# A two-layer MetaFormer with a selective scan: last states enter by a ScalarE product, GpSimd makes one C product more, deeper row buffers, later gates

## The chip, the cores and the metric

The kernel runs on one core of a Trainium2 chip. The metric is the device time of one launch in microseconds (us), the median of several runs. The engines are TensorE (PE in the profile, PEld for its weight loads), VectorE (DVE), ScalarE (ACT), GpSimd (POOL) and SyncE (SP), which issues nearly all transfers here. Each engine works through its own queue in order; between engines, semaphores tell when data is ready or a buffer is free.

## The reference, cut to what matters

The input is two images of 96 channels, 128 x 128 pixels. Layer 0 normalizes each pixel over the channels, runs four Mamba blocks (over rows, rows backwards, columns, columns backwards), joins their outputs and adds them; layer 1 has a 3 x 3 convolution instead. After each comes a small quantized feed-forward part. Nearly all of the time is spent in the Mamba blocks, of which this is the core:

```python
dt = jax.nn.softplus(dt_raw @ dt_w.T + dt_b)
A = -jnp.exp(A_log)
def step(h, t):
    dt_t, u_t, B_t, C_t = t
    dA = jnp.exp(dt_t[:, :, None] * A)
    h = dA * h + dt_t[:, :, None] * B_t[:, None, :] * u_t[:, :, None]
    y = jnp.einsum('bds,bs->bd', h, C_t)
    return (h, y)
_, ys = jax.lax.scan(step, h0, xs)
y = ys.transpose(1, 0, 2) + Dp * xc
y = y * jax.nn.silu(z)
return y @ outp_w.T
```

There are 16384 tokens per sequence, 192 inner channels and 16 states per channel.

## The kernel before, in words

For each of the two images: `normalize` (layer norm, and a copy of the image in row order and in column order to DRAM), `mamba`, then `ffn_and_conv`. The change touches `mamba` alone, and one argument where the program is made.

`mamba` treats the four directions as two pairs (one row and one column direction each, both forwards or both backwards). A pair has 2 x 192 = 384 channels, which fill three groups `g` of 128 partitions. Tokens are cut into 32 tiles of 512; one tile of one pair is a *step*, so there are 64 steps per image and 128 in the run. Within a step, a *unit* is one group and two states: `units` has 3 x 8 = 24 of them, numbered here 0 to 23; units 0, 8 and 16 start a group. Two units share a *quad* of four states.

For one unit the engines do this:
- SP loads the rows of B and of C for a quad from a DRAM scratch (`bcd`), broadcast to 128 partitions: 1 MB each (`row_tile`, L331 to L338). B rows are fetched 3 quads ahead (`B_AHEAD`), C rows 2 (`C_AHEAD`), in buffers of one more than that: 4 and 3.
- GpSimd multiplies the B rows by dt·u for a whole quad, in place (`b_part`, L339). Where the step is not the first of a sequence (i > 0), it also adds to the first token's column what the last step's states leave: `entry` (L303) makes exp(dt·A) of the first token on ScalarE, L342 multiplies it by the last states `hst`, L343 adds it into the row.
- ScalarE makes dA, two exponentials of 512 tokens into PSUM (`decay`, L349). The pool `ps_w` has three such buffers of two banks each; y and a tile for everything else take the two banks left.
- DVE runs two scans, one per state (`scan`, L353), then multiplies the states by the C rows (L441). In the units of `BY_POOL`, 0, 4, 8, 12, 16 and 20, the scan writes its states into the row tile instead of dA, and GpSimd makes the C product (`by_pool`, L360).
- ScalarE saves the last token's states (L442), and TensorE sums the products over states by multiplying with an identity into y (`sums`, L357). At the end of a group DVE multiplies y by the gate `sz` (`gated`, L364).

What a step needs beforehand (convolution, gates, dt, the scratch rows) is the `prologue` of the step before: a list `at` of small parts, each with a unit number counted from 24 units before the step, and a place: 0 is before scan 0 of the unit, 1 is after scan 1. On ScalarE these are copies out of PSUM, and three activations that need other tables and so have two table loads each: silu of the gates behind unit 7 (L259), silu of the convolution before unit 11, softplus of dt behind unit 17 (L293).

The order on every engine is the order in which the program is written (`in_order`). The loop over k, one pass per unit, sets it: transfers and GpSimd's B product for later units, parts with place 0, scan 0 of unit k, `behind(k - 1)` (C product, state copy, sums, and in a group's first unit the gate of the group before, L446, and the first matmul into a new y, L448), dA of unit k + 2, scan 1 of unit k, the C rows' transfer, parts with place 1. GpSimd's C product of unit k is registered for the pass k + 1, its sums for the pass k + 3. With three dA buffers, dA of unit k + 2 goes where that of unit k - 1 was.

## Time and profile before

| | |
|---|---|
| median of 3 runs | 11548.93 us (11548.27 to 11549.71) |
| the profiled execution | 11556.77 us, its span 11555.0 us |
| granted TensorE clock, mean | 0.989 |
| step | about 79.1 us, 128 of them |
| DVE scans (L353) | 6144 of about 1.21 us |
| DVE C products (L441) | 2304 of 1.21 us |
| GpSimd B products (L339) | 1536 of 4.52 us |
| GpSimd C products (L360) | 768 of 2.35 us |
| ScalarE exponentials (L349) | 6144 of 0.69 us |
| ScalarE entry (L303), GpSimd L342 and L343 | 372 of 0.29, 372 of 0.22, 1488 of 0.20 us |
| row transfers | 3072 of 1 MB, 7.4 us from issue to landing (median) |

Times in the profile are counted from the start of the span. A group line gives the line of the kernel, the engine, the operation, output and inputs, how many there are, busy time and the mean of one, then the idle time of the engine just before them and what ended it. In a timeline, "x2" merges two instructions that follow each other; the bracket is the idle time before and what ended it. In a table of stretches each row gives the busy time of each engine in it, then the granted clock, the share of the DMA engines' time, and GB/s.

### The profile page before, as it was taken

Reading aid. Unit: us, or ns where it says so; the run is one execution under the profiler, and the core shown is the slowest. Engines: PE = TensorE matmul, PEld = TensorE weight load, DVE = VectorE, ACT = ScalarE, POOL = GpSimd, SP = SyncE. Lnnn points to the kernel's source line nnn. Section 1 sums busy time; section 2 is a strip of 40 time slices with the busy share of each in tenths; the row PEclk is TensorE's granted clock in tenths of the full one; section 3 lists DMA queues with packets and bytes.
Section 4 is the critical chain, followed back from the end, with each engine's and each line's share of the span. In section 5 each row is a group of like instructions: output and inputs, shape, how many; then the busy total and the mean of one; then the engine's idle time right before and its main releaser. Section 6 shows DMA issues by size and latency. Waiting matters only on the chain. (4 is left out here: it accounts for less than half of the span.)

```text
span 11555.0 us, 94102 instructions
## 1 busy us (share of the span) xinstructions
PE 10435.0 (90%) x24208; PEld 3971.4 (34%) x24208; DVE 10421.6 (90%) x10127; ACT 7901.7 (68%) x13564; POOL 9672.3 (84%) x4700
## 2 busy tenths in 40 slices
PE   7999999999999999989989999999999999999899
PEld 2333333333333333333323333333333333333333
DVE  6999999999999999994469999999999999999944
ACT  6767767677677677665567677677676776776655
POOL 5999999999999999991159999999999999999911
PEclk8999999999999999999989999999999999999999
DMA  7888888888888888880068888888888888888800
GB/s 263 335 329 333 333 332 332 330 331 333 329 332 333 330 331 333 329 322 19 26 243 334 328 331 334 330 333 333 333 331 329 332 332 329 331 333 329 319 13 13
DMA packets 540755, 3416.96 MB, mean 296 GB/s; under 512 B 67532, under 2 KB 68652, under 8 KB 143832
## 3 DMA queue, kind: packets, MB, share of 16 engines
q1 hardware_dynamic: 539960, 3410.16, 76.8%
q8 instruction: 196, 3.21, 0.1%
q14 instruction: 343, 2.81, 0.1%
q0 software_dynamic: 256, 0.79, 0.0%
HBM read 3289.04 MB, written 54.53 MB: 289 GB/s over the span
## 5 line engine op out<-in xcount | busy, mean ns | idle before, releaser
L339 POOL TENSOR_TENSOR row<-dtu,row 128x2048 f32<-128x2048 f32 x1536 | 6948.9, 4524 | 283.3 <-DMA row<-bcd 281.6
L357 PE MATMUL y<-row,ident 128*128 128x512 f32 x12288 | 5690.6, 603 | 700.0 <-DVE row L441 699.9
L353 DVE TENSOR_TENSOR_SCAN da<-da,row 128x512 f32<-128x512 f32 x4608 | 5456.9, 1214 | 38.9 <-ACT da L349 5.2
L349 ACT ACTIVATE da<-dt,amat 128x512 f32<-128x512 f32 x6144 | 4246.9, 691 | 170.2
L357 PEld LDWEIGHTS y<-row,ident 128*128 128x128 f32 x12288 | 2256.8, 190 | 4008.4 <-issue 2243.5
L441 DVE TENSOR_TENSOR row<-da,row 128x1024 f32<-128x1024 f32 x2304 | 2776.7, 1205 | 70.2 <-DMA row<-bcd 70.0
L442 ACT COPY hst<-da 128x2 f32<-128x2 f32 x2304 | 368.9, 160 | 2652.2 <-DVE row L441 2649.3
L360 POOL TENSOR_TENSOR row<-row,row 128x1024 f32<-128x1024 f32 x768 | 1807.4, 2353 | 223.0 <-DVE row L353 147.5
L353 DVE TENSOR_TENSOR_SCAN row<-da,row 128x512 f32<-128x512 f32 x1536 | 1852.4, 1206 | 91.9 <-POOL row L339 84.1
L211 PE MATMUL misc<-xa,inx 96*64 96x512 f32 (+1 forms) x2048 | 946.1, 605 | 50.0 <-ACT mix L239 26.8
L211 PE MATMUL misc<-xb,inx 96*64 96x512 f32 (+1 forms) x2048 | 952.3, 608 | 33.6 <-ACT hst L442 24.2
L564 POOL TENSOR_TENSOR acc<-acc,y 96x512 f32<-96x512 f32 x128 | 147.4, 1151 | 991.5 <-DVE y L563 991.5
L298 POOL TENSOR_TENSOR dtu<-dt,xc 128x512 f32<-128x512 f32 x384 | 487.4, 1269 | 106.0 <-DMA xb<-xnc 99.8
L576 PE MATMUL pc<-pad,kw 96*96 96x512 f32 x1152 | 566.4, 593 | 0.0
L211 PEld LDWEIGHTS misc<-xa,inx 96*64 96x64 f32 (+1 forms) x2048 | 327.3, 165 | 581.2 <-issue 438.0
L448 PE MATMUL y<-xc,dmat 128*128 128x512 f32 x768 | 419.5, 628 | 103.6 <-DVE sz L364 103.6
L374 PE MATMUL misc<-sz,gmat 128*96 128x512 f32 x1024 | 484.1, 595 | 0.0
L284 PE MATMUL misc<-rows,dtw 12*128 12x512 f32 x768 | 434.3, 645 | 50.6 <-ACT dt L289 37.9
L364 DVE TENSOR_TENSOR sz<-y,sz 128x512 f32<-128x512 f32 x384 | 264.6, 689 | 229.5 <-PE y L357 198.0
L136 DVE TENSOR_TENSOR xq<-xm,rs 96x512 fp8e5<-96x512 f32 x128 | 87.9, 687 | 392.2 <-ACT rs L132 392.2
L211 PEld LDWEIGHTS misc<-xb,inx 96*64 96x64 f32 (+1 forms) x2048 | 316.5, 164 | 361.9 <-issue 214.1
L372 PE MATMUL misc<-acc,ident 96*96 96x512 f32 x512 | 387.6, 842 | 57.3 <-ACT sz L247 53.8
(76 smaller groups left out, 7449.9 us busy)
## 6 DMA issues: line engine op xcount, KB each, us to landing
row<-bcd SPq DMA_DIRECT2D x3072, 1024.0 KB, 7.4
xc<-mix SPq DMA_DIRECT2D x256, 128.0 KB, 5.4
sz<-mix SPq DMA_DIRECT2D x256, 128.0 KB, 8.9
xa<-xnr SPq DMA_DIRECT2D x124, 193.1 KB, 8.6
xb<-xnc SPq DMA_DIRECT2D x124, 193.1 KB, 8.7
bcd<-rows SPq DMA_DIRECT2D x128, 128.0 KB, 9.5
acc<-in_x_dram SPq DMA_DIRECT2D x16, 768.0 KB, 5.7
xnr<-xn SPq DMA_DIRECT2D x16, 768.0 KB, 4.3
```

Of the source, the lines that this page charges most:

```text
L211: nc.tensor.matmul(ps[rows, :], w(PAIRS[pi][d], k, lo, hi), src[d][:, k : k + T], **se)
L284: nc.tensor.matmul(d["ps"], w, d["rows"][0 : 2 * RK, :], start=True, stop=True)
L298: nc.gpsimd.tensor_tensor(dtu, d["dt"][:, g, :], d["xc"][:, g, :], ALU.mult)
L339: nc.gpsimd.tensor_tensor(b, d["dtu"][g][:, None, :].broadcast_to((128, 4, T)), b, ALU.mult)
L349: nc.scalar.activation(da[:, j, :], d["dt"][:, g, :], AF.Exp, scale=amat[:, pi, g, s + j : s + j + 1])
L353: nc.vector.tensor_tensor_scan(h[:, j, :], da[:, j, :], b[:, j, :], 0.0, ALU.mult, ALU.add)
L357: nc.tensor.matmul(y, ident, c[:, j, :], start=False, stop=s + j == S - 1)
L360: nc.gpsimd.tensor_tensor(c, h, c, ALU.mult)
L374: nc.tensor.matmul(d["po"], gmat[:, pi, 2 * g - 2 + k, :], d["yg"][g - 1 + k], start=False, stop=k == 1)
L441: nc.vector.tensor_tensor(c, h, c, ALU.mult)
L448: nc.tensor.matmul(y, dmat[:, pi, g, :], d["xc"][:, g, :], start=True, stop=False)
L576: nc.tensor.matmul(pc, kw[:, t, :], rows, start=t == 0, stop=t == 8)
```

## The change

Four things change in `mamba`.

The last states enter elsewhere. `entry`, the tile `enter` and the three lines L341 to L343 are gone. In `decay`, where i > 0, two further ScalarE instructions multiply the first token's dA, in PSUM, by the saved state of that unit; the scan then starts from 1.0 instead of 0.0, so its first product is that value.

`BY_POOL` also holds (1, 4), which is unit 10: seven C products of 24 are GpSimd's.

The row buffers no longer follow from the read-ahead: `ROW_BUFS` gives 5 for B and 4 for C, at read-aheads of 3 and 2 as before. The space that is set aside for the descriptors of GpSimd's transfers goes down to 2048 bytes.

`behind(k - 1)` moves behind scan 1 of unit k where unit k - 1 is the first of a group and in `BY_POOL` (units 0, 8, 16), so the gate and the first matmul into the next y come one scan later, and the state copy behind dA of unit k + 2.

```diff
+ROW_BUFS = (5, 4)
-BY_POOL = tuple((g, s) for g in range(3) for s in (0, 8))
+BY_POOL = tuple((g, s) for g in range(3) for s in (0, 8)) + ((1, 4),)
...
-                    if i > 0:
-                        at += [((20, 24, 29)[g], 1, partial(entry, g))]
...
-                t = gen.tile([128, 4, T], F32, name=f"row{k}", bufs=ahead + 1)
+                t = gen.tile([128, 4, T], F32, name=f"row{k}", bufs=ROW_BUFS[k])
...
-                if i > 0:
-                    if s == 0:
-                        nc.gpsimd.tensor_tensor(enter[:, g, :], enter[:, g, :], hst[:, g, :], ALU.mult)
-                    nc.gpsimd.tensor_tensor(b[:, :, 0], b[:, :, 0], enter[:, g, s : s + 4], ALU.add)
...
-            def decay(pi, d, g, s):
+            def decay(pi, i, d, g, s):
...
+                if i > 0:
+                    for j in range(2):
+                        nc.scalar.activation(da[:, j, 0:1], da[:, j, 0:1], AF.Copy, scale=hst[:, g, s + j : s + j + 1])
                 return da
...
-                nc.vector.tensor_tensor_scan(h[:, j, :], da[:, j, :], b[:, j, :], 0.0, ALU.mult, ALU.add)
+                nc.vector.tensor_tensor_scan(h[:, j, :], da[:, j, :], b[:, j, :], float(i > 0), ALU.mult, ALU.add)
...
+            def begins(k):
+                return 0 <= k < total and units[k % nu][1] == 0 and units[k % nu] in BY_POOL
...
-                if 0 < k <= total:
+                if 0 < k <= total and not begins(k - 1):
                     behind(k - 1)
                 feed_decay(k + AHEAD)
                 if k < total:
-                    scan(1, da, b, hs[k])
+                    scan(steps[n][1], 1, da, b, hs[k])
+                if begins(k - 1):
+                    behind(k - 1)
...
-    nc = bacc.Bacc("TRN2", target_bir_lowering=False, num_devices=1)
+    nc = bacc.Bacc("TRN2", target_bir_lowering=False, num_devices=1, dynamic_dma_scratch_size=2048)
```

More of the change, by code (lines that the diff above doesn't have):

```diff
@@ L194, in mamba @@
             hst = one.tile([128, NG, S], F32, name="hst")
-            enter = one.tile([128, NG, S], F32, name="enter")
             acc_w = acc.rearrange("c (h w) -> c w h", w=W)
@@ L299, in dt_u @@
                     d["dtu"].append(dtu)
-                def entry(g):
-                    nc.scalar.activation(enter[:, g, :], amat[:, pi, g, :], AF.Exp, scale=d["dt"][:, g, 0:1])
                 first = pi == 0 and i == 0
@@ L327, in prologue, with row_tile @@
                 return sorted(at, key=lambda p: p[:3])
-            def row_tile(d, g, s, k, ahead):
-                t = gen.tile([128, 4, T], F32, name=f"row{k}", bufs=ahead + 1)
+            def row_tile(d, g, s, k):
+                t = gen.tile([128, 4, T], F32, name=f"row{k}", bufs=ROW_BUFS[k])
                 src = d["bcd"][k, s // 4] if g == 1 else d["bcd"][k, s // 4, g // 2 : g // 2 + 1]
@@ L336, in row_tile, with b_part @@
                 return t
-            def b_part(i, d, g, s, b):
+            def b_part(d, g, b):
                 nc.gpsimd.tensor_tensor(b, d["dtu"][g][:, None, :].broadcast_to((128, 4, T)), b, ALU.mult)
-                if i > 0:
-                    if s == 0:
-                        nc.gpsimd.tensor_tensor(enter[:, g, :], enter[:, g, :], hst[:, g, :], ALU.mult)
-                    nc.gpsimd.tensor_tensor(b[:, :, 0], b[:, :, 0], enter[:, g, s : s + 4], ALU.add)
-            def decay(pi, d, g, s):
+            def decay(pi, i, d, g, s):
                 da = ps_w.tile([128, 2, T], F32, name="da")
@@ L349, in decay, with scan @@
                     nc.scalar.activation(da[:, j, :], d["dt"][:, g, :], AF.Exp, scale=amat[:, pi, g, s + j : s + j + 1])
-                return da
-            def scan(j, da, b, h):
-                nc.vector.tensor_tensor_scan(h[:, j, :], da[:, j, :], b[:, j, :], 0.0, ALU.mult, ALU.add)
+                if i > 0:
+                    for j in range(2):
+                        nc.scalar.activation(da[:, j, 0:1], da[:, j, 0:1], AF.Copy, scale=hst[:, g, s + j : s + j + 1])
+                return da
+            def scan(i, j, da, b, h):
+                nc.vector.tensor_tensor_scan(h[:, j, :], da[:, j, :], b[:, j, :], float(i > 0), ALU.mult, ALU.add)
             def sums(s, y, c):
@@ L413, in mamba, with fetch @@
             bs, cs, das, hs, quads = {}, {}, {}, {}, {}
-            def fetch(k, n, ahead, m):
+            def fetch(k, n, m):
                 if k < total:
-                    t = row_tile(state[k // nu], *units[k % nu], n, ahead)
+                    t = row_tile(state[k // nu], *units[k % nu], n)
                     m[k], m[k + 1] = t[:, 0:2, :], t[:, 2:4, :]
@@ L425, in feed @@
                     n = k // nu
-                    b_part(steps[n][1], state[n], *units[k % nu], quads.pop(k))
+                    b_part(state[n], units[k % nu][0], quads.pop(k))
             def feed_decay(k):
@@ L430, in feed_decay, with gate_before @@
                     n = k // nu
-                    das[k] = decay(steps[n][0], state[n], *units[k % nu])
+                    das[k] = decay(*steps[n], state[n], *units[k % nu])
             ys = {}
+            def gate_before(k):
+                pn, pu = divmod(k - 1, nu)
+                gated(steps[pn][0], state[pn], units[pu][0], ys.pop(k - 1))
+            def begins(k):
+                return 0 <= k < total and units[k % nu][1] == 0 and units[k % nu] in BY_POOL
             def behind(k):
@@ L444, in behind @@
                     if k > 0:
-                        pn, pu = divmod(k - 1, nu)
-                        gated(steps[pn][0], state[pn], units[pu][0], ys.pop(k - 1))
+                        gate_before(k)
                     y = ps_y.tile([128, T], F32, name="y")
@@ L464, in mamba @@
                 for k in range(ahead):
-                    fetch(2 * k, n, ahead, m)
+                    fetch(2 * k, n, m)
             feed(0)
@@ L474, in mamba @@
                 if k % 2 == 0:
-                    fetch(k + 2 * B_AHEAD, 0, B_AHEAD, bs)
+                    fetch(k + 2 * B_AHEAD, 0, bs)
                     feed(k + AHEAD)
@@ L481, in mamba @@
                     hs[k] = b if (g, s) in BY_POOL else da
-                    scan(0, da, b, hs[k])
-                if 0 < k <= total:
+                    scan(steps[n][1], 0, da, b, hs[k])
+                if 0 < k <= total and not begins(k - 1):
                     behind(k - 1)
@@ L486, in mamba @@
                 if k < total:
-                    scan(1, da, b, hs[k])
+                    scan(steps[n][1], 1, da, b, hs[k])
+                if begins(k - 1):
+                    behind(k - 1)
                 if k % 2 == 0:
-                    fetch(k + 2 * C_AHEAD, 1, C_AHEAD, cs)
+                    fetch(k + 2 * C_AHEAD, 1, cs)
                 issue(k, 1)
```

## The prediction

> **What bounds the kernel now.** The page's first part comes first: three engines are near full.

> ```profile
> PE 10435.0 (90%) x24208; PEld 3971.4 (34%) x24208; DVE 10421.6 (90%) x10127; ACT 7901.7 (68%) x13564; POOL 9672.3 (84%) x4700
> ```

> DVE's 90% is the highest where it counts: its spans overlap by 0.09 us (two scans of 1.21 take 2.33), so the Mamba stage is DVE instructions 1.12 apart. A step is 24 units (0 to 23), a unit is two states, and the stage is 2 x 64 steps of about 79.1 us. What a step loses stands in the table of waits.

> ```profile
> DVE sz L364 <- PE y L357: 198.0, 207, 3.1
> DVE row L441 <- DMA row<-bcd: 70.0, 121, 1.3
> ```

> Over 128 steps that is 1.55 us a step before the gates and 0.55 before a C product. I then cut 79.09 us, from scan 0 of unit 13 to the same scan a step later, into four stretches. The three gates in it (2965.58, 2990.99 and 3017.77, in units 17, 1 and 9) tell the units.

> ```profile
> core 0: us, PE busy (x) PEld busy (x) DVE busy (x) ACT busy (x) POOL busy (x), PEclk, DMA share, GB/s
> 2950.73:2974.04 23.31, 20.21 (x43) 7.00 (x42) 22.13 (x20) 18.20 (x32) 22.64 (x13) 1.00 0.97 365
> 2974.04:3011.55 37.51, 34.86 (x87) 13.36 (x87) 36.80 (x35) 20.97 (x42) 35.55 (x19) 1.00 0.71 289
> 3011.55:3019.50 7.95, 7.59 (x20) 2.97 (x17) 7.43 (x8) 7.68 (x12) 6.07 (x4) 1.00 1.01 413
> 3019.50:3029.82 10.32, 9.37 (x23) 3.90 (x22) 10.18 (x10) 9.01 (x13) 10.24 (x4) 1.00 0.92 351
> ```

> In order of time the rows are C (scan 0 of unit 13 to that of 20), D (to scan 1 of unit 7 of the next step), A (to scan 0 of 10) and B (to scan 0 of 13). ScalarE is 68% busy over all, but 7.68 of 7.95 us in A. Its timeline there:

> ```profile
> 3011.66 0.16 ACT L442 COPY hst<-da 128x2 f32<-128x2 f32 x1 [1.35 <-DVE row L441]
> 3011.86 1.42 ACT L349 ACTIVATE da<-dt,amat 128x512 f32<-128x512 f32 x2
> 3013.29 1.28 ACT L259 ACT_TABLE_LOAD   x1
> ...
> 3017.86 0.17 ACT L442 COPY hst<-da 128x2 f32<-128x2 f32 x1
> 3017.91 1.43 ACT L349 ACTIVATE da<-dt,amat 128x512 f32<-128x512 f32 x2
> ...
> 3028.37 1.42 ACT L349 ACTIVATE da<-dt,amat 128x512 f32<-128x512 f32 x2
> ```

> And DVE's:

> ```profile
> 3010.41 1.22 DVE L441 TENSOR_TENSOR row<-da,row 128x1024 f32<-128x1024 f32 x1 [0.65 <-DMA row<-bcd]
> ...
> 3017.77 0.69 DVE L364 TENSOR_TENSOR sz<-y,sz 128x512 f32<-128x512 f32 x1 [0.52 <-PE y L357]
> 3018.38 2.33 DVE L353 TENSOR_TENSOR_SCAN da<-da,row 128x512 f32<-128x512 f32 x2
> ...
> 3029.82 3.61 DVE L353 TENSOR_TENSOR_SCAN da<-da,row 128x512 f32<-128x512 f32 x3
> ```

> The reader is to see two coincidences. In A, dA of unit 10 ends at 3019.34 and its scan starts at 3019.50. In B, dA of unit 13 ends at 3029.79 and its scan starts at 3029.82. Both times a silu with two table loads (4.07 us) stood ahead of that dA, and the chain began when a C product freed one of three dA buffers. So ScalarE is already the clock of A and B, with almost no slack.

> [...] L303 (16 elements, pointer scale) takes 294 ns and what follows starts 0.20 after it (2978.41 to 2978.61). [...]

> **The change, part by part.**

> Part 1, GpSimd's (1,4), unit 10. DVE loses one L441 a step, 1.12. But its neighbours, the two scans of unit 11, then follow each other, and such a pair costs 2.38, not 2.24 (unit 21: 2976.27 row scan, three scans taking 3.59 from 2977.40), as scan 1 waits for scan 0: net -0.98. GpSimd gains 2.35 (L360) and loses 12 L343 and 3 L342, in steps of 0.15 and 0.30: 2.7 less. Its queue at units 8 to 14 becomes product, b, product, b, product. Unit 8's product starts when its scans end, 3016.1; + 2.31 + 4.47 (what lies between the starts of L360 and of what follows it, and the same for L339) puts b of units 12 and 13 at 3022.9, or 1.9 later if the 1.80 us that GpSimd now waits there for a row at 3013.49 stays. The scan that needs it comes at 3026.0 (the sums below). Nothing waits; the cover is 1.2 to 3.1 us.

> Part 2, later gates. The gate moves behind scan 1, 1.12 later. In C its wait was 1.15 (2965.58), with 0.09 of lost overlap; in A 0.52; in D's gate (2990.99) none. All go, and each of the three pairs of scans now costs 0.13 as in part 1. With it move the state copy of the group's first unit, now behind two exponentials on ScalarE (they don't wait for it: that unit's states lie in a row, not in dA), and PE's matmul into the next y. That waits as much longer, with the group's sums and the next input products queued behind it on PE; PE is idle 5 us a step waiting for C products (699.9 us in all), and in A a convolution occupies it until 3021.7 anyway. GpSimd's product of that unit is issued in the same place as before.

> Part 3, row buffers 5 and 4. SP waits 6879.4 us for PE at L335, the release of C buffers; with one buffer beyond the read-ahead and one more, that release is two units old. D shows 0.71 DMA share, so there is room to load early, and the 0.65 (+0.09 overlap) at 3010.41 goes. I take -0.74; the bound above is nothing. A loss would come from small transfers landing behind more rows in flight: the scratch rows (bcd, 9.5 us to landing) are issued at unit 14 and first read for a row issued at unit 18, 4 x 3.36 = 13.4 us on, so 4 us more are covered. The smaller descriptor area touches only four GpSimd transfers: nothing.

> Part 4, the entry products. Off POOL's path, and L303 off ScalarE's. Added, in the 62 of 64 steps with i > 0: two one-element ACTIVATEs per unit, PSUM to PSUM, pointer scale, 48 x 124 = 5952 over the run. The scan waits for the second. In the built program the first waits on ScalarE's own semaphore for the exponential, the second on nothing. In the trace an exponential that waits so starts 0.03 past the end of the one before, 0.72 after its start. Nobody in the trace does such a copy. [...] So from the first exponential: 0.72 + 0.72 + (0.24 - 0.09) + 0.24 = 1.83 against 1.42: **0.42 more per unit**. Bounds: 0.25 (each 0.16, like L442) and 0.60 [...]. Queued behind the waiting copy on ScalarE are the silu, the state copies, the PSUM copies of the input products (PE and SP's mix transfers wait for those, units ahead of need) and the next dA, for which DVE waits.

> **Sum for one step**, unit by unit in the stretches:
> - A: the chain holds dA(9), silu, gate copy, dA(10): 3019.34 + 2 x 0.42, + 0.03: 8.66 against 7.95, +0.71. DVE alone would need 6 x 1.12 + 0.13 + 0.60 = 7.45: the gate's 0.52 goes, and the wait for ScalarE that takes its place is 1.2.
> - B: dA(12), conv copy, silu, dA(13): + 2 x 0.42, minus 0.11 because the state copy between now reads a row (0.08 to the next start instead of 0.19): +0.73. DVE alone would need 10.32 - 0.98 - 0.23 = 9.1, so the product given to GpSimd buys nothing here.
> - C: -1.24 + 0.13 = -1.11. ScalarE's dA(20) behind the softplus ended 2971.54; + 3 x 0.42 = 2972.80, DVE comes at 2972.93. It just fits.
> - D: -0.74 + 0.13 = -0.61.

> Together -0.28 a step, x 124 = -35 us; the four steps without copies gain 0.13 + 0.11 + 1.11 + 0.61 = 1.96 each, -8. In all **-43 us**. The profiled execution took 11556.77 (span 11555.0), 7.8 above the median 11548.93; against the median the forecast is 11506 us.

> **Rivals.**
> - *Nearly free copies*, 0.25 a unit: A +0.37, B +0.39: -0.96 a step, **11422**. For it: L442's 160 ns. Against: no pointer operand there.
> - *ScalarE doesn't set A and B at all*: -0.50 -1.21 -1.11 -0.61 = -3.43 a step, **11110**. For it: ScalarE's 68%. Against: the two coincidences; GpSimd, whose 74.50 us of this step would be 74.2, would then be next.
> - [...] 0.49 a unit: +0.09 a step, **11552**, no change.
> - *Serial copies* (slower): the two copies of a unit don't overlap, 0.60 a unit. Place: scan 0 of units 10, 13 and now 20, where C's room of 0.13 is used up and three of them count. Per step -0.28 + 4 x 0.04 + 7 x 0.14 = +0.86: **11648**. It decides from 0.48 a unit on, where the sum is zero.
> - *The C row still comes late* in D, because A to C run the DMA engines at 0.92 to 1.01: +0.46 a step, **11601**.

> **How the numbers follow.** Forecast 0.42 (own range 11470 to 11540), free copies 0.18, ScalarE not binding 0.05, full price 0.10, serial 0.15, late row 0.10. Within 0.2% (23 us, about what a measurement can tell) lie the full price and some of the forecast. Faster: 0.18 + 0.05 + 0.34 = 0.57; same: 0.08 + 0.08 = 0.16; slower 0.27. The range 11415 to 11635 leaves out the 11110 and most of the serial case.

> **What would show it.** After: scans of units 10 and 13 idle before ScalarE, about 1.2 and 1.9 us, so a large "DVE da L353 <- ACT" where there were 5.2 us in all; gates without a wait for y; no DMA wait before the C product; the copies near 240 ns, 150 apart; ACT busy up by about 1300 us (5952 x 0.24, less 109 of L303). Wrong if scans never wait for ScalarE, or if the gates still wait.

## The result, and the profile after

The changed kernel takes 11723.36 us (median of 4 runs, 11717.96 to 11728.64) against 11549.32 us for the kernel before in the same series (11548.27 to 11557.76): ratio 1.0149, 95% interval 1.0131 to 1.0167. It is slower by 174 us; the forecast was 11506, faster by 43. The profiled execution of the changed kernel took 11728.64 us, its span is 11726.9 us, and the mean granted TensorE clock is 0.969 (0.989 before).

The busy times come first again. The page of the changed kernel, first part:

```profile
PE 10576.8 (90%) x24208; PEld 4022.6 (34%) x24208; DVE 10328.4 (88%) x9999; ACT 8966.8 (76%) x19144; POOL 9612.4 (82%) x2968
```

DVE has 93 us less to do, GpSimd 60 less, ScalarE 1065 more (the forecast of about 1300 counted the two copies of a unit without their overlap). TensorE has the same 24208 matmuls as before and yet 142 us more of busy time: its instructions take longer. (A matmul of the program is two records in the trace: x4 are the two sums of one unit.) The groups of instructions of the changed kernel show that the direct parts of the change came out as priced:

```profile
L439 DVE TENSOR_TENSOR row<-da,row 128x1024 f32<-128x1024 f32 x2176 | 2617.9, 1203 | 0.1
...
L340 ACT ACTIVATE da<-da,hst 128x1 f32<-128x1 f32 x5952 | 1160.7, 234 | 97.3
```

The C products no longer wait for a row transfer (0.1 us of idle time, 70.2 before), and a copy takes 234 ns. The table of waits of the changed kernel (engine, its line, whom it waits for: us in total, times, longest):

```profile
PE misc L363 <- ACT hst L440: 300.1, 126, 2.5
...
DVE sz L355 <- PE y L348: 233.7, 246, 3.3
DVE da L344 <- ACT da L340: 230.5, 122, 1.9
...
PE misc L266 <- ACT xc L259: 205.8, 128, 3.6
...
PE misc L284 <- ACT rows L272: 145.7, 124, 1.2
...
DVE row L344 <- ACT da L340: 82.0, 124, 0.7
...
DVE row L344 <- ACT hst L440: 37.2, 54, 1.1
```

The two lines of DVE's scans behind L340 are the expected ones: 1.89 us before unit 13 and 0.66 before unit 10. The gates' wait for y (L355) should have gone and has grown from 198.0 to 233.7. (0.45 us a step of it lies in A, in unit 9; that part costs nothing, because the scan of unit 10 behind it waits for ScalarE anyway: 0.45 + 0.66 is about the 1.2 of the forecast.) Three lines on TensorE are new in size: it waits for ScalarE at L266 (the product that makes the rows of B, C and dt; 7.1 us in all before), at L284 (the products for dt; 1.3 before) and at L363 (the projection; the line names the state copy L440, but in the timeline of ScalarE the gate copy L247, 0.60 us from 3020.95, ends 0.06 before the projection starts at 3021.61; that copy empties the one PSUM tile `misc`, which the projection writes next). The table of waits of the kernel before, where the projection is L372:

```profile
PE misc L372 <- ACT sz L247: 53.8, 126, 0.4
...
PE misc L266 <- ACT xc L259: 7.1, 2, 3.6
```

What this does in one step, first on DVE. The timeline of the changed kernel, DVE, units 10, 13 and 17 of one step:

```profile
2986.61 1.22 DVE L344 TENSOR_TENSOR_SCAN row<-da,row 128x512 f32<-128x512 f32 x1 [0.66 <-ACT da L340]
...
2997.70 3.61 DVE L344 TENSOR_TENSOR_SCAN da<-da,row 128x512 f32<-128x512 f32 x3 [1.89 <-ACT da L340]
...
3014.27 0.69 DVE L355 TENSOR_TENSOR sz<-y,sz 128x512 f32<-128x512 f32 x1 [1.60 <-PE y L348]
```

And TensorE in the same step:

```profile
2994.47 2.81 PE L266 MATMUL misc<-xc,bcw 128*96 128x512 f32 x6 [1.60 <-ACT xc L259]
2997.13 3.60 PE L348 MATMUL y<-row,ident 128*128 128x512 f32 x8
3001.91 1.12 PE L284 MATMUL misc<-rows,dtw 12*128 12x512 f32 x2 [1.18 <-ACT rows L272]
3002.96 3.51 PE L348 MATMUL y<-row,ident 128*128 128x512 f32 x4
...
3012.25 1.98 PE L348 MATMUL y<-row,ident 128*128 128x512 f32 x4
```

The same four sums take 3.51 us at 3002.96 and 1.98 at 3012.25. The clock record of the trace has 0.5 from 3003.27 to 3006.69, one stretch of 3.41 us. TensorE waited for ScalarE twice just before, 1.60 and 1.18 us. The table of stretches of the changed kernel over C of this step (scan 0 of unit 13 to that of 20) shows both, the longer time and the clock:

```profile
core 0: us, PE busy (x) PEld busy (x) DVE busy (x) ACT busy (x) POOL busy (x), PEclk, DMA share, GB/s
2997.70:3021.63 23.93, 19.35 (x39) 6.47 (x37) 22.25 (x21) 20.09 (x44) 21.37 (x7) 0.93 0.77 321
```

C was 23.31 us before and forecast 1.11 shorter. The clock records of the whole trace hold 546 us at 0.5 inside the Mamba stage, where the kernel before has 41: 70 stretches begin in units 14 and 15, and 54 in unit 20, of the 124 steps with copies.

Means over nearly all steps with copies, worked out from the start times of the scans, in the four stretches of the prediction (us per step, difference to the kernel before; before: A 8.16, B 10.32, C 23.32, D 37.40):

| | A | B | C | D | sum |
|---|---|---|---|---|---|
| forecast | +0.71 | +0.73 | -1.11 | -0.61 | -0.28 |
| the changed kernel | +0.60 | +0.77 | +0.38 | -0.15 | +1.61 |

A and B are right. C misses by 1.49 and D by 0.46. C loses its time at the gate of unit 17. D loses it elsewhere, at scan 0 of the next step's unit 0. A half clock in unit 20 lengthens the projection and the sums (in one such step the twelve records of sums behind the projection take 5.99 us from 2943.89; at full clock, at 3024.26, 5.31), so TensorE's input product in unit 21 ends late; ScalarE's gate copy (L247) waits for that product, 362.0 us in all (249.9 in the kernel with everything but the copies, `no_entry` below), and dA of unit 0 stands behind this copy. That is the last line of the first table of waits above, where the state copy behind this dA is named, with 54 waits, as many as half-clock stretches begin in unit 20: in steps with such a stretch D takes 37.68 us, in the others 36.88.

(The sum over 124 steps, 200 us, is more than the 172 us between the two spans: the steps without copies gain.)

### The profile page after: what moved, and what is told of

It reads as the page before. It is cut to its first block, busy times and chain, and to the rows that moved or that the text cites. A ratio compares the mean times of both kernels' runs of the same rounds, so it can differ in the third digit from the quotient of the medians.

```text
span 11726.9 us, 98197 instructions
## 1 busy us (share of the span) xinstructions
PE 10576.8 (90%) x24208; PEld 4022.6 (34%) x24208; DVE 10328.4 (88%) x9999; ACT 8966.8 (76%) x19144; POOL 9612.4 (82%) x2968
## 4 chain that ended last, share of the span: by engine, by line
ACT 33%; DVE 32%; PE 23%; issue 11%; DMA 1%; POOL 0%; DVEq 0%; SPq 0%; POOLq 0%; ACTq 0%
DVE da L344 17%; ACT da L337 14%; PE y L348 8%; DVE row L439 8%; DVE row L344 6%; PE pc L575 4%; ACT da L340 3%; ACT L260 3%; PE misc L284 3%; PE xm L123 2%; PE v L129 2%; ACT xc L259 2%; ACT sz L259 2%; ACT L259 1%; PE misc L365 1%
## 5 line engine op out<-in xcount | busy, mean ns | idle before, releaser
L348 PE MATMUL y<-row,ident 128*128 128x512 f32 x12288 | 5785.9, 613 | 127.6 <-DVE row L439 127.2
L344 DVE TENSOR_TENSOR_SCAN da<-da,row 128x512 f32<-128x512 f32 x4352 | 5199.6, 1216 | 271.6 <-ACT da L340 230.5
L348 PEld LDWEIGHTS y<-row,ident 128*128 128x128 f32 x12288 | 2321.6, 194 | 3450.3 <-issue 2468.7
L351 POOL TENSOR_TENSOR row<-row,row 128x1024 f32<-128x1024 f32 x896 | 2107.3, 2352 | 784.9 <-DVE row L344 684.8
L439 DVE TENSOR_TENSOR row<-da,row 128x1024 f32<-128x1024 f32 x2176 | 2617.9, 1203 | 0.1
L344 DVE TENSOR_TENSOR_SCAN row<-da,row 128x512 f32<-128x512 f32 x1792 | 2164.2, 1208 | 190.6 <-ACT da L340 82.0
L440 ACT COPY hst<-da 128x2 f32<-128x2 f32 x2176 | 358.3, 165 | 1308.1 <-DVE row L439 1303.2
L340 ACT ACTIVATE da<-da,hst 128x1 f32<-128x1 f32 x5952 | 1160.7, 234 | 97.3
L363 PE MATMUL misc<-acc,ident 96*96 96x512 f32 x512 | 388.2, 843 | 378.8 <-ACT hst L440 300.1
L284 PE MATMUL misc<-rows,dtw 12*128 12x512 f32 x768 | 461.3, 682 | 164.7 <-ACT rows L272 145.7
L365 PE MATMUL misc<-sz,gmat 128*96 128x512 f32 x1024 | 556.3, 671 | 0.0
L266 PE MATMUL misc<-xc,bcw 128*96 128x512 f32 x768 | 365.6, 612 | 205.8 <-ACT xc L259 205.8
L445 PE MATMUL y<-xc,dmat 128*128 128x512 f32 x768 | 422.5, 632 | 111.0 <-DVE sz L355 111.0
L355 DVE TENSOR_TENSOR sz<-y,sz 128x512 f32<-128x512 f32 x384 | 263.0, 685 | 233.8 <-PE y L348 233.7
```

Source lines behind the costliest of these rows:

```text
L284: nc.tensor.matmul(d["ps"], w, d["rows"][0 : 2 * RK, :], start=True, stop=True)
L340: nc.scalar.activation(da[:, j, 0:1], da[:, j, 0:1], AF.Copy, scale=hst[:, g, s + j : s + j + 1])
L344: nc.vector.tensor_tensor_scan(h[:, j, :], da[:, j, :], b[:, j, :], float(i > 0), ALU.mult, ALU.add)
L348: nc.tensor.matmul(y, ident, c[:, j, :], start=False, stop=s + j == S - 1)
L351: nc.gpsimd.tensor_tensor(c, h, c, ALU.mult)
L365: nc.tensor.matmul(d["po"], gmat[:, pi, 2 * g - 2 + k, :], d["yg"][g - 1 + k], start=False, stop=k == 1)
```

## The experiments

Theory 1: the mistake is on TensorE. ScalarE's delay makes TensorE wait, in order, for silu, the copied rows and the gate copy; its clock halves, its sums into y are late, and the gate of unit 17 (C) and what follows unit 20 (D) come late. The rivals: the copies delay DVE's own chain in C; or row transfers and buffers are late; or another part of the change is at fault. Ratios are to the kernel before in the series of each run, in which it took 11545 to 11554 us.

**The parts, one at a time.** The first run is the kernel before with the new entry of the last states alone, the second is the changed kernel with the old entry (`entry`, `enter`, L341 to L343 as before).

```diff
@@ entry_only, against the kernel before
...
+                if i > 0:
+                    for j in range(2):
+                        nc.scalar.activation(da[:, j, 0:1], da[:, j, 0:1], AF.Copy, scale=hst[:, g, s + j : s + j + 1])
...
@@ no_entry, against the changed kernel
-                if i > 0:
-                    for j in range(2):
-                        nc.scalar.activation(da[:, j, 0:1], da[:, j, 0:1], AF.Copy, scale=hst[:, g, s + j : s + j + 1])
...
+                        at += [((20, 24, 29)[g], 1, partial(entry, g))]
...
+                    nc.gpsimd.tensor_tensor(b[:, :, 0], b[:, :, 0], enter[:, g, s : s + 4], ALU.add)
```

> The kernel before with part 4 alone: the entry products on ScalarE, nothing else changed. Theory 1 (ScalarE's copies make its silu and row copies late, TensorE waits for them in order, idles, and its clock halves, so y is late): stretches A and B grow by 0.71 and 0.84 us a step, and on top of that half-clock windows cost 1 us or more a step; clock under 0.98, time 11850 to 11950 us. Rival 2 (the slow clock and the late y come of the later gates or of the product on GpSimd): A and B alone, x 124 steps: 11741 us, clock 0.989.

> The changed kernel without part 4: last states enter as before (one activation per group on ScalarE, L342 and L343 on GpSimd), with the seventh product on GpSimd, row buffers 5 and 4 and the later gates. Theory 1: no late silu, clock 0.989 again; a step as the changed kernel's one step without copies, 77.24 us, or GpSimd's own 77.8 us of work: 11330 to 11390 us. Rival 2 (gates or the product to blame): gates still wait for y over 1 us in unit 17, clock 0.97, 11650 us or more.

Measured: 11962.95 us, ratio 1.0358 (1.0341 to 1.0375), with the new entry alone; 11317.6 us, 0.9798 (0.9783 to 0.9812), with everything but it. Both lie 12 or 13 us outside the range of Theory 1 (11850 to 11950, and 11330 to 11390) and far from the rival's. So the entry costs about 400 us in either surrounding (11963 - 11549 and 11723 - 11318), and the other three parts gain 232. Without the entry no gate waits, and the stretches are A -0.26, B -0.09, C -0.89, D -0.52.

The two cheaper sets of parts were then run as well: `gates_rows` has the later gates and the deeper row buffers alone, `pool_only` GpSimd's seventh product alone.

```diff
@@ pool_only, against the kernel before
-BY_POOL = tuple((g, s) for g in range(3) for s in (0, 8))
+BY_POOL = tuple((g, s) for g in range(3) for s in (0, 8)) + ((1, 4),)
@@ gates_rows, against the kernel before
+ROW_BUFS = (5, 4)
...
-                if 0 < k <= total:
+                if 0 < k <= total and not begins(k - 1):
                     behind(k - 1)
...
+                if begins(k - 1):
+                    behind(k - 1)
...
```

> The kernel before, with unit (1,4) added to GpSimd's C products and nothing else. Theory 1 (ScalarE is the clock of units 9 to 12, where this product lies): DVE loses 0.98 us a step but then waits for dA of unit 13, so no change, 11530 to 11565 us. Rival (DVE is the bound there): -0.98 x 128 = -125, about 11425 us. Rival (GpSimd, which gains 2.35 us a step and in this kernel still does the entry additions, becomes late): above 11600 us, with scans that wait for L339.

> The kernel before, with the later gates and the deeper row buffers; the last states enter as before and GpSimd makes six products. Theory 1: all of the gain of the version without the new entry (11318 us, -231) lies in the gate of unit 17 (-1.11 a step) and the C row in front of unit 8 (-0.61), and nothing in units 9 to 12: so -1.72 x 128 = -220, 11310 to 11350 us. Rival (the seventh GpSimd product carries part of that gain): 11400 us or more.

`pool_only` takes 11578.54 us (1.0021, 1.0012 to 1.0029), `gates_rows` 11305.74 us (0.9785, 0.9771 to 0.9800), a little above and a little below the ranges of Theory 1. The seventh product buys nothing where ScalarE is the clock: B changes by -0.11. C changes by +0.25: there the wait of the third theory shows, for GpSimd's additions of the last states (scans wait 57.8 us in all for L343, 7.1 before), though smaller than it said. Its table of waits has, as a sign of who was waited for in B instead:

```profile
DVE da L353 <- ACT da L349: 125.6, 135, 2.1
```

That is about 1 us a step of waiting for dA, where the kernel before had 5.2 us in all: nearly the 0.98 that DVE no longer needs. The later gates and the buffers carry the whole gain: C -1.11, D -0.51, A -0.26. `gates_rows` is the fastest kernel of this study.

**Is it TensorE's clock?** The changed kernel plus eight matmuls a step, which add zero to y and stand just ahead of the products that wait for ScalarE.

```diff
@@ after_warm, against the changed kernel
+                    nc.tensor.matmul(ys[k][:, 0:384], zero, dmat[:, 0].rearrange("p g c -> p (g c)"), start=False, stop=False)
...
+                if 0 < k < total and steps[n][1] > 0:
+                    warm(k - 2, {12: 3, 14: 2, 19: 3}.get(u, 0))
                 issue(k, 0)
```

> The changed kernel with 8 more matmuls a step that add zeros to y, placed in TensorE's queue ahead of the three instructions that wait for ScalarE (3 in unit 12 before the rows matmuls, 2 in unit 14 before dt, 3 in unit 19 before the projection), so that TensorE is busy while it would wait. Theory 1: the half-clock windows go, clock 0.985 or more, a step takes the 79.3 us of the changed kernel's steps without such a window: 11560 to 11590 us although work was added. Rival 3 (y is late because the sums stand in the queue behind what waits for ScalarE, at any clock): 11720 us or more.

11536.61 us (0.9986, 0.9979 to 0.9992), clock 0.991, 17 us at half clock in the Mamba stage instead of 546; Theory 1 had 11560 to 11590. More work on TensorE makes the kernel 187 us faster. The gate's wait in its table of waits:

```profile
DVE sz L355 <- PE y L348: 87.5, 246, 3.1
```

C is -0.76 now and D -0.51. So 1.14 of C's miss and 0.36 of D's are the halved clock, 1.50 x 124 = 186 us. Of C 0.35 is left, which the last run below explains.

The same filler in `entry_only`:

```diff
@@ entry_warm, against entry_only: the filler of after_warm
+                if 0 < k < total and steps[n][1] > 0:
+                    warm(k - 2, {12: 3, 14: 2, 19: 3}.get(u, 0))
```

> The kernel before, with the new entry alone, and eight matmuls a step that add zero to y, ahead of the products for which TensorE waits on ScalarE. Without these matmuls it took 11963 us, +414. Theory 1 (ScalarE's delay of units 9 and 12, 1.44 a step = 179 us, and the rest through TensorE's halved clock): 11720 to 11790 us with a granted clock of about 0.99. Rival (the rest comes from row transfers and buffers that are late): 11880 us or more even at full clock.

12048.34 us (1.0427, 1.0411 to 1.0442): the expectation of Theory 1 (11720 to 11790) fails although the clock is at 0.989, and the time is in the rival's range. The timeline of TensorE in this kernel shows why the run doesn't decide (L390 is the filler; the left out lines have no idle time of TensorE either):

```profile
3505.34 2.10 PE L390 MATMUL y<-dmat,zero 128*128 128x384 f32 x6
...
3511.56 1.45 PE L390 MATMUL y<-dmat,zero 128*128 128x384 f32 x4
...
3521.64 1.98 PE L349 MATMUL y<-row,ident 128*128 128x512 f32 x4
```

From 3501.80 to the gate of unit 17 TensorE never stops: the 3.5 us of filler are more than the waits for ScalarE that they fill (196.7 us at L283 and 159.4 at L364 in `entry_only`, 2.9 a step), and the gate, in its early place, waits 2.76 us in this step. What `entry_only` loses beside the clock is to be read from its own table of waits:

```profile
DVE sz L356 <- PE y L349: 370.1, 246, 6.2
...
DVE row L433 <- DMA row<-bcd: 136.6, 129, 2.1
```

With the small row buffers the wait for late C rows doubles (70.0 before), GpSimd's for B rows too (563.4, 281.6 before), D is +0.57, and 259 us at half clock are part of C's +1.17. How C splits there was not settled.

**Without ScalarE's copies.** The last states enter as the scan's first value, read by DVE itself.

```diff
@@ after_init, against the changed kernel
-                if i > 0:
-                    for j in range(2):
-                        nc.scalar.activation(da[:, j, 0:1], da[:, j, 0:1], AF.Copy, scale=hst[:, g, s + j : s + j + 1])
...
-                nc.vector.tensor_tensor_scan(h[:, j, :], da[:, j, :], b[:, j, :], float(i > 0), ALU.mult, ALU.add)
+                first = hst[:, g, s + j : s + j + 1] if i > 0 else 0.0
+                nc.vector.tensor_tensor_scan(h[:, j, :], da[:, j, :], b[:, j, :], first, ALU.mult, ALU.add)
```

> The changed kernel with the last states given to the scan as its initial value (a [128,1] operand) instead of the two copies on ScalarE; nothing enters on GpSimd either. Theory 1: 77.24 us a step, 11310 us, clock 0.989. If the pointer costs each scan time on DVE, 48 x 0.06 us a step or so, 11650 to 11700 us, with scans longer than 1.216 us. Rival 2: clock 0.97 and 11650 us or more with scans as long as before.

11575.02 us (1.0019, 1.0011 to 1.0026), between the two times that Theory 1 gave (11310, or 11650 to 11700 with dearer scans). The copies and the half clock are gone, but each scan is dearer. The groups of this kernel (the second line is the scans of the steps without last states):

```profile
L342 DVE TENSOR_TENSOR_SCAN da<-da,hst,row 128x512 f32<-128x512 f32 x4216 | 5291.1, 1276 | 118.9 <-ACT da L337 88.5
...
L342 DVE TENSOR_TENSOR_SCAN da<-da,row 128x512 f32<-128x512 f32 x136 | 162.5, 1216 | 9.2 <-ACT da L337 7.4 <-POOL row L331 0.8
```

0.06 us for each of 48 scans would be 2.9 us a step if DVE were the bound everywhere; a step takes 79.53, 2.1 more than in `no_entry`, since in A and B ScalarE leaves DVE room.

**Which copies?** Two complementary kernels: the copies in units 9 to 13 only, where ScalarE is the clock of A and B, and in all other units only. Where there is no copy the last states of these units are left out.

```diff
@@ after_9to13 (and after_not9to13, with "not" ahead of the condition), against the changed kernel
-                if i > 0:
+                if i > 0 and 9 <= 8 * g + s // 2 <= 13:
                     for j in range(2):
```

> The changed kernel with the copies in units 9 to 13 alone; in the other 19 units the last states are left out (the scan starts from 1). Theory 1 (here lies ScalarE's direct clock: +1.09 at unit 9 and +0.84 at unit 12, less 0.42 that GpSimd's lateness at units 7 and 15 gives back): 77.45 + 1.5 = 78.95 us a step, 124 x 1.5 = 186 above the 11318 of no copies: 11500 us, gates without a wait. Rival (these copies also bring TensorE's half clock): 11640 to 11700 us, half-clock stretches in units 14 and 20 as in the changed kernel.

> The changed kernel with the copies in all units but 9 to 13, where the last states are left out (the scan starts from 1). Theory 1 (outside units 9 to 13 DVE is the clock and covers the copies): 11315 to 11350 us. Rival (the copies of units 14 to 20 make TensorE wait and halve its clock by themselves): 11430 to 11500 us, with a wait at the gate of unit 17.

With units 9 to 13: 11491.79 us (0.9949, 0.9934 to 0.9963), stretches +0.58, +0.75, -1.11, -0.52. That is the forecast's sum, -0.30 a step against -0.28, and nearly its time, 11506. All of ScalarE's delay in A and B is in it, and no half clock beyond the 41 us of the kernel before. Its table of waits:

```profile
DVE da L344 <- ACT da L340: 227.6, 122, 1.9
...
PE misc L363 <- ACT hst L440: 196.6, 126, 1.6
```

With the others: 11440.88 us (0.9904, 0.9889 to 0.9919), where Theory 1 had 11315 to 11350 and the rival 11430 to 11500: the rival holds. C is -0.76 and D +0.30; 114 stretches at half clock begin in unit 20, none in 14 or 15. The same waits:

```profile
PE misc L363 <- ACT hst L440: 307.1, 126, 2.5
...
DVE row L344 <- ACT hst L440: 83.7, 116, 2.2
```

The last line is the wait at unit 0 of the next step; the gates wait 88.1 us in all. So the copies outside A and B, which the forecast held to be covered, cost 1.0 us a step by way of TensorE (78.48 against 77.45 without copies). And the two halves don't add up: +1.45 and +1.03 a step alone, +3.35 together, and only together do they bring the half clock of unit 14. The wait at L363 is in large part not the copies' doing: 53.8 us in the kernel before, it is 196.4 in `gates_rows` and 196.5 in `no_entry`, about 1.6 a step, so it comes with the later gates and row buffers, and there no half clock begins in unit 20. With the 0.9 us a step that the copies outside A and B add, 114 do.

**How late must ScalarE be?** One copy per unit instead of two (the odd state of each unit doesn't enter).

```diff
@@ after_half, against the changed kernel
-                    for j in range(2):
+                    for j in range(1):
```

> The changed kernel with one copy per unit instead of two: the even state of each unit enters, the odd one is left out (its scan starts from 1). The unit costs about 0.27 on ScalarE instead of 0.42. Theory 1: 4 x 0.15 = 0.6 a step less in units 9 to 12, and shorter waits of TensorE, so most of the half clock goes too (1.35 a step): 11723 - 124 x 1.95 = 11480 if all of it goes, up to 11650 us if none does. Rival (half clock does not depend on how long ScalarE is late): 11640 to 11660 us with as many stretches at half clock as in the changed kernel.

11450.96 us (0.9913, 0.9896 to 0.9929), below the range expected: A and B are 0.32 and 0.33 cheaper than with two copies, 20 stretches at half clock are left in units 19 and 20, and none in 14 and 15. Half of the copies give back 272 of the 406 us that all of them cost: the loss is not in proportion to the delay.

**Moving the waits.** The changed kernel with TensorE's rows and dt products one unit later; the last copy of dt moves so that it stays ahead of the softplus.

```diff
@@ after_later, against the changed kernel
-                at += [(12, 0, rows), (13, 1, rows_out), (14, 0, rows_to_dram)]
+                at += [(13, 0, rows), (13, 1, rows_out), (14, 0, rows_to_dram)]
...
-                for g, k in enumerate((14, 24, 25) if first else (14, 15, 16)):
+                for g, k in enumerate((14, 24, 25) if first else (15, 16, 17)):
-                    at += [(k, 0, partial(dt_in, g)), (k + 1, 0, partial(dt_out, g))]
+                    at += [(k, 0, partial(dt_in, g)), (k + 1, 0, partial(dt_out, g)) if first or g < 2 else (k, 1, partial(dt_out, g))]
```

> The changed kernel, with the product that makes the rows of B, C and dt one unit later (unit 13 instead of 12) and the three products for dt one unit later too (units 15 to 17), so that TensorE comes to them when ScalarE has made their input. Nothing is added. Theory 1 (TensorE's waits for ScalarE bring the half clock): the waits at L266 and L284 of 1 to 2 us go, fewer stretches at half clock, 11560 to 11650 us. Rival (the half clock comes from something else than these waits, or only the one at unit 19 to 20 counts): 11700 to 11740 us.

11864.52 us (1.0270, 1.0255 to 1.0285): slower, against both expectations. The half clock at unit 14 is gone as meant, and no wait of the gate of unit 17 is left. C is -0.49 all the same: 0.62 is now lost at scan 0 of unit 20, where the forecast had seen 0.13 of room. ScalarE's copies for dt and the softplus behind them are later too, and with them the gate copy for which the projection waits. TensorE in one step of this kernel:

```profile
3380.68 1.98 PE L348 MATMUL y<-row,ident 128*128 128x512 f32 x4
3386.11 2.02 PE L363 MATMUL misc<-acc,ident 96*96 96x512 f32 x2 [3.45 <-ACT hst L440]
3387.92 3.62 PE L365 MATMUL misc<-sz,gmat 128*96 128x512 f32 x4
```

It idles for 3.45 us (2.35 in the changed kernel), then the projection's first part takes 2.02 us where it took 1.10. Nearly every step has the half clock here (125 stretches in units 19 and 20), 6.8 us long as a rule, and D is +1.89. The wait was moved, not taken away.

**GpSimd's product, with the new entry.** The changed kernel with six products of GpSimd.

```diff
@@ after_six, against the changed kernel
-BY_POOL = tuple((g, s) for g in range(3) for s in (0, 8)) + ((1, 4),)
+BY_POOL = tuple((g, s) for g in range(3) for s in (0, 8))
```

> The changed kernel without GpSimd's seventh product: six C products, as before; later gates, deeper row buffers and the new entry stay. Theory 1 (ScalarE clocks units 9 to 12, so the product given to GpSimd buys nothing there): 11690 to 11750 us. Rival (moving that product shifts the phase of TensorE's waits): 11650 us or less, with fewer stretches at half clock.

11812.97 us (1.0227, 1.0212 to 1.0242), slower than either theory said. So the seventh product, which buys nothing in B, gains 90 us here. A and B are as with seven (+0.58, +0.86), C is +1.04: 109 stretches at half clock begin in units 14 and 15 instead of 70. Why the sums of unit 10, which come two units earlier here, let the clock fall more often was not tried.

**What stands ahead of the half clock?** In the Mamba stage of the changed kernel the clock records at 0.5 are 130 stretches, 100 of 3.41 us and 30 of 6.83. In the 3.41 us ahead of them TensorE's longest wait is one of 1.18 to 1.19 us at L284 (the 70 that begin in units 14 and 15), of 2.34 to 2.50 at L363 (the 54 of unit 20) or of 2.04 at L445 (the other six). I cut the Mamba stage at full clock into stretches of 3.41 us, in line with the records, added up the matmuls' busy time as a share of each, and asked whether the next stretch has the half clock:

```
                 followed by half clock       not followed
                 stretches  highest share     lowest share
before                   9           0.43             0.43
changed kernel         130           0.71             0.42
after_six              178           0.71             0.41
after_later            134           0.46             0.43
after_half              26           0.41             0.41
entry_only              46           0.64             0.46
```

Idle time doesn't tell the two kinds apart: in the changed kernel stretches with up to 71% of busy matmuls were followed by the half clock, and others with 42% were not. In all the 70 stretches ahead of the half clock of units 14 and 15 stand products for dt, which have 12 rows where the sums have 128. That their narrowness counts was only a guess, so it was tested: the same products over all 96 rows of their input, the 84 others with a weight of zero.

```diff
@@ after_96rows, against the changed kernel
-    dtw = const("dtw", (2 * RK, 2, NG * 128))
+    dtw = const("dtw", (BCO + NBC, 2, NG * 128))
...
-                    nc.tensor.matmul(d["ps"], w, d["rows"][0 : 2 * RK, :], start=True, stop=True)
+                    nc.tensor.matmul(d["ps"], w, d["rows"], start=True, stop=True)
...
-    dtw = np.zeros((2 * RK, 2, 2 * DI), f)
+    dtw = np.zeros((BCO + NBC, 2, 2 * DI), f)
```

> The changed kernel; the three products for dt run over all 96 rows of their input, with weights of zero for the 84 rows that aren't dt's, instead of over 12 rows. The same number of instructions and the same results. [...] Theory 1 [...]: the half-clock stretches of units 14 and 15 go (70 of them), those of unit 20 stay in half of the steps or more, so a step takes 79.3 to 80.13 us: 11560 to 11660 us. Rival (only idle time counts, and a product of 12 rows is as good as one of 96): 11700 to 11740 us, as many half-clock stretches as in the changed kernel.

11587.19 us (1.0035, 1.0022 to 1.0048), 136 us less than the changed kernel (132 by the two ratios, since the kernel before took 11545.04 in this series), with the same number of instructions. No half clock begins in units 14 and 15 any more; 83 stretches do in units 19 and 20 (54 in the changed kernel). C is -1.11, the forecast's number to the hundredth, and D +0.30. Steps with no half clock at all take 78.92 us, 0.27 less than the mean of the kernel before. C's remaining 0.35 went too, though the wait for the rows is still 142.0 us in all. TensorE's timeline of this kernel shows it, beside the lines of the changed kernel above:

```profile
574.14 1.12 PE L284 MATMUL misc<-rows,dtw 96*128 96x512 f32 x2 [1.15 <-ACT rows L272]
575.11 1.88 PE L348 MATMUL y<-row,ident 128*128 128x512 f32 x4
...
581.80 1.02 PE L284 MATMUL misc<-rows,dtw 96*128 96x512 f32 x2
582.67 1.88 PE L348 MATMUL y<-row,ident 128*128 128x512 f32 x4
```

The wait of 1.15 us is as long as before (1.18), and the four sums behind it take 1.88 us instead of 3.51. Four sums behind a product of 12 rows take 1.98 even at full clock: in the trace of the changed kernel around a product of 12 rows four starts of matmuls in a row come 0.52 to 0.53 us apart, and 0.43 here. For the last dt product, which runs without a wait ahead of it, that is four times 0.09, about the 0.35 of C that was left at full clock.

## Why the prediction was wrong

Of the steps of the prediction these were right:
- **ScalarE is the clock of A and B.** +0.60 and +0.77 measured, +0.71 and +0.73 forecast; DVE's wait before unit 13 is 1.89 us, forecast 1.9; `pool_only` gains nothing.
- **The price of the copies.** 234 ns (the forecast's 0.24 us was the author's estimate), two of them in 0.39 (0.15 apart). In units 9 and 12 one copy costs 0.27 and the second 0.16 per unit (`after_half`: A and B together gain 0.65 over four dA), 0.43 in all against 0.42 (the forecast's own sum, 1.83 less 1.42, is 0.41). The rivals of free and of serial copies fall.
- **Part 3.** C products wait 0.1 us for rows; D without half clock is -0.51 or -0.52, about 0.1 short of the forecast.
- **Part 2 and part 1 in themselves.** The later gates give C -1.11 where the states enter as before (`gates_rows`) or in units 9 to 13 alone; the product given to GpSimd buys nothing in B, as said, and its GpSimd cover held in A and B (with the old entry it did not hold in C: +0.25 in `pool_only`).

Wrong: the sum for C, "-1.24 + 0.13 = -1.11", of which it says "It just fits", with "All go" in part 2. It compared ScalarE's dA with DVE only. The step under it is in part 4: behind the waiting copy are queued "the PSUM copies of the input products (PE and SP's mix transfers wait for those, units ahead of need)". They were not units ahead of need. Silu's output, the copied rows and the gate copy are each waited for by a product on TensorE (0.1, 0.0 and 0.4 us a step before, 1.6, 1.2 and 2.4 after), and the sums into y, on which the gate depends, stand behind these products in the same queue. Part 2 had seen TensorE's queue and written its idle 5 us a step off as cover. That idle time was spread over waits for C products (699.9 us in all before, 127.2 after); now it was gathered in three places, at L363 a large part of it came with the later gates and row buffers themselves, and behind two of them, L284 and L363, the half-clock stretches begin (70 in units 14 and 15, 54 in unit 20). The forecast had no term for the clock: the rows of its table of stretches all showed 1.00.

The sum for D failed in the same way: it took ScalarE and TensorE to be on time at the next step's unit 0.

The miss of 1.89 us a step then divides: A and B -0.07, C's half clock 1.14, C's changes between 12 and 128 rows 0.35 (which hurt only once ScalarE is late: with the copies in units 9 to 13 alone the gate doesn't wait), D's half clock 0.36, and 0.10 by which part 3 was oversized. Clock and row changes together are 1.85 x 124 = 229 us, about the distance from forecast to result (11506 to 11723). That these two could be removed was shown on different kernels: `after_warm` has no half clock and keeps the 0.35, `after_96rows` loses the 0.35 and the half clock of unit 14 but keeps that of unit 20. No run has removed both, nor were the waits of L363 taken away without a filler.

The rivals of the prediction don't hold either. None had TensorE as the one that is late: the slower ones, 11601 and 11648, rest on a late C row and on the price of the copies, and neither was the cause.

## What to carry to other kernels

When an engine off the critical path gets more work, follow every consumer of what it makes, in queue order, to the end: here a ScalarE delay of 0.4 us per unit cost 1.7 us a step at the scans that wait for it (A and B, against `no_entry`; four times the 0.42 of the forecast), and as much again (C and D) through TensorE products that nobody had counted, whose followers in the queue feed the path. A TensorE at 90% busy with a granted clock of 1.00 in the stretches looked at isn't safe cover: look at how its idle time is spread, and at narrow products beside it. Here the halved clock, which cost C 1.14 us a step, came behind waits of 1.18 us beside products of 12 rows, and not behind 1.15 us beside products of 96 (`after_96rows`). A test for this is cheap: put matmuls that change nothing into the wait, or widen a narrow product with zero weights, and see whether the kernel gets faster. The filler must fit into the wait: in `entry_warm` it didn't, and that run decided nothing.
